# A four-layer kernel whose last layer is a recurrence: the lower layers of the first two blocks in two halves, slots by readiness, and another order of loading

## The chip, the core and the metric

The kernel runs on one core of a Trainium2 chip. The metric is the time of one launch in device microseconds; before the change the median of three runs is 1330.2 us (1329.89 to 1331.93).

## The reference

x is (8, 512, 256) in float32: 8 sequences, 512 time steps, 256 features. A condition vector of 256 features goes with each sequence. Four layers follow one another, each added to its input:

```python
x = x + moe(x, cond)         # shared silu gate unit (512 hidden) + top 2 of 8 experts (128 hidden each, gelu)
x = x + haar(x, cond)        # Haar levels, one gate per feature on all levels
x = x + adapted(x, cond)     # down, gelu, up; each with a rank-8 part that cond generates
x = x + gru(x, cond)         # h0 = cond

def gru(X, h0):              # per time step
    Z = sigmoid(x Wxz + H Whz + b);  R = sigmoid(x Wxr + H Whr + b)
    C = tanh(x Wxh + (R * H) Whh + b)
    H = Z * H + (1 - Z) * C
    Y = H Whq + bhq
```

As every level of the Haar layer has the same gate, the kernel computes that layer as one factor per sequence and feature (`lr2`). Only the recurrent layer links the time steps.

## The kernel before

**Blocks.** The 512 steps are cut into 16 windows (blocks) of 32 steps; a block of 8 sequences is 256 columns. For each block `window_jobs` adds *jobs* to lists: `hidden` (32 products of x with the first weights, two feature halves for each of 8 shared and 8 expert parts, into two PSUM banks `hp`), the sigmoid or Erf on ACT (tile `sig`, a ring of three), products on DVE (`lin`, `g`, `gl`; `gl` is a ring of three), the gate product on POOL (`g`, L594), and `into_acc` (24 products into the bank `acc`). Then come the *lower layers*: x1 on DVE (L612), x2 = x1 times `lr2` on POOL (L621), and twice `adapted`: a low-rank product into `misc` (`low_in`), the mask `u` on DVE (L649), four products with `wsq_a` and two with `low_out` into `low`; between the two an Erf on ACT (L691) and `mid` on DVE (L700). At the end x is updated on DVE (L713) and turned into `xt`, time major, by two copies on POOL (L722). Each product is a `quads` call (L453): four 32-column tiles at once, 8 matmuls.

**The order.** No scheduler on the chip chooses; the program is written out once, in order for each engine. A `Job` has an engine, the jobs that it depends on, the buffers that it uses and a planned duration (`TAKES`, `takes`, `lag` for a transfer). A `Ring` of more than one buffer gives them out only in the order in which the tiles were asked for when the jobs were made. Before the recurrence `Jobs.run` plays a clock and gives each engine the first ready job of its list `queues`. It runs until block 0's `acc`, the generated low-rank weights (`got_low_in`) and the recurrent weights (`wx`, `wh`) are there by its plan, and then until block 0's `xt` is; then `AHEAD` = 3 more PE jobs are placed.

**The prologue.** x of the first four blocks, `sw13`, `rw1`, `sw2`, `wsq_a`, `rw2`, eight pieces of `w2` (1 MB each, a ring of five buffers), `wx`, `wh` and the rest of x are loaded by the SP queue in this order. `route` computes the gates of four blocks (24 small DVE operations in a chain), which go through HBM (`comb_d`) and come back broadcast to all partitions (`bc`). A chain of small products and operations on cond makes `hid`; `generate` (L1023) multiplies it with the pieces of `w2`; a copy and a transpose on PE make `low_out` and `low_in`.

**The recurrence.** Step s writes the products of the state with `wh` (`recur`, L1115, tiles `grh` and `gz`), activations (L1281), DVE transposes (L1295), and two scans per step (L1372) that give the new state `s_h`. Between them `fill` puts jobs of the blocks to come into slots: on PE up to one job before the candidate's products (if `behind(s)` says that the plan's pace is missed, or if none are left) and one or two after them. Five steps ahead, `project` (also L1115, with `wx`) adds a group's input products; it needs `xt` of its block, and asserts that the jobs that make it have been placed. Outputs of chunks of 16 steps (`output_jobs`) are `urgent` for chunks below `HELD` = 12, and otherwise in the list `last`, which is used only when all blocks' PE jobs are placed.

```python
def behind(s, by=0):
    return (
        any(j.done is None for j in ends[1])
        or jobs.left("PE") > all_left * (LAST - s) / (LAST + LEAD) + by
    )
...
jobs.fill("PE", now + 0.5, 1 if behind(s) or late(s) else 0)
...
two = behind(s, 8) or ahead % 2 == 0 and behind(s)
jobs.fill("PE", now + 1.44, 2 if two else 1)
```

Of the kernel before, what the change touches and what calls it, by code (L numbers as in the profile page):

```python
# [50 lines left out]
LOW = (3, 2), (0, 1)  # L51
EARLY = 4
# [9 lines left out]
AHEAD = 3  # L62
# [74 lines left out]
class Jobs:  # L137


    def __init__(self):  # L140
        self.queues = {e: [] for e in TAKES}
        self.urgent = {e: [] for e in TAKES}
        self.last = {e: [] for e in TAKES}
        self.small = {e: [] for e in TAKES}
        self.clock = {e: 0.0 for e in TAKES}
        self.now = 0.0

# [9 lines left out]
    def fill(self, eng, now, most, ahead=40, then=None, of=None):  # L157

        n = 0
        while n < most:  # L160
            last = [] if self.left("PE") else self.last[eng]
# [17 lines left out]
    def run(self, until):  # L179

        while any(j.done is None for j in until):
            for eng, at in self.clock.items():
                if at <= self.now:
                    job = next((j for j in self.queues[eng] if j.ready(self.now)), None)
                    if job is not None:
                        self.queues[eng].remove(job)
# [13 lines left out]
def cond_resid_kernel(  # L200
# [69 lines left out]
    r_sig = ring("sig", [P, NT], 3)  # L270
    r_lin = ring("lin", [P, NT], 2)
    r_g = ring("g", [P, NT], 6)
    r_gl = ring("gl", [P, NT], 3)
# [36 lines left out]
    jobs = Jobs()  # L310

# [35 lines left out]
    def load_x(n, mb, some=None):  # L347
# [8 lines left out]
        a, b = (i * WS for i in some)  # L356
        for k in range(KC):
            got = load(t[:, k, :, a:b], xs[:, k, :, t0 + a : t0 + b], mb)
# [5 lines left out]
    load_x(0, 0.25, (0, 1))  # L364
    sw13_sb = const.tile([P, 2, KC, HS], F32, name="sw13_sb")
    got_sw13 = [load(sw13_sb[:, g], rows_of(sw13[g]), 0.5) for g in range(2)]
    load_x(0, 0.4, (1, EARLY))
    got_vec = load(vec, vecs, 0, eng="ACT")
    got_b2 = load(b2[: 4 * R], bias2.rearrange("q (r d) -> (q r) d", d=C), 0, eng="ACT")
    rw1_sb = const.tile([P, KC, E, P], F32, name="rw1_sb")  # L370
    got_rw1 = load(rw1_sb.rearrange("p k e h -> p k (e h)"), rows_of(rw1), 1.0)
    sw2_sb = const.tile([P, HC, C], F32, name="sw2_sb")
    got_sw2 = load(sw2_sb, rows_of(sw2), 0.5)
    wsq_a = const.tile([P, KC, 5, C], F32, name="wsq_a")
# [5 lines left out]
    r_w2 = Ring(pro.enter_context(tc.tile_pool(name="w2q", bufs=5)), "w2", [P, R * C], 5)  # L380
# [84 lines left out]
    def window_jobs(w, routed, xt, via_pool=False):  # L465
# [18 lines left out]
        def fetch(i):  # L484
# [12 lines left out]
                lag=LAG,  # L497
# [27 lines left out]
        def hidden(lazy, n, lhs, got):  # L525
            last = None
            for k in range(KC):
                last = mm(
                    lazy,
                    n,  # L530
                    lambda k=k: lhs(k),
                    lambda k=k: x[:, k],
                    k == 0,
                    [last, got, got_x[w]],
                )
            return last
# [3 lines left out]
        for m in range(HC):  # L540
            h, sig, lin, g = bank(), Lazy(r_sig), Lazy(r_lin), Lazy(r_g)
            j1 = hidden(h, 0, lambda k, m=m: sw13_sb[:, 0, k, ts(m, P)], got_sw13[0])
            j3 = hidden(h, 1, lambda k, m=m: sw13_sb[:, 1, k, ts(m, P)], got_sw13[1])
# [26 lines left out]
        for e2 in range(0, E, 2):  # L570
            h = bank()
            for n in range(2):
                e = e2 + n
                j = hidden(h, n, lambda k, e=e: rw1_sb[:, k, e, :], got_rw1)
# [15 lines left out]
                    [h, sig, gl],  # L590
                )
# [15 lines left out]
        x1, x2 = Lazy(r_x1), Lazy(r_x2)  # L607
        done = []
        for m in range(KC):
            d = add(  # L610
                "DVE",
                lambda m=m: stt(  # L612
                    bt(x1.get()[:, m]), bt(acc.get()[:, m]), THIRD, x[:, m], ALU.mult, ALU.add
                ),
                [order[0]],
                [acc, x1],
            )
# [4 lines left out]
                        x2.get()[:, m].rearrange("p (b t) -> p b t", t=WS),  # L622
                        x1.get()[:, m].rearrange("p (b t) -> p b t", t=WS),
                        lr2[:, m, :].rearrange("p (b o) -> p b o", o=1).broadcast_to([P, B, WS]),
# [3 lines left out]
                    [x1, x2],  # L628
                )
            )  # L630

        def adapted(out, n, src, base, deps, first):

            lu = Lazy(r_m)
            last = None
            for k in range(KC):
                last = mm(
                    lu,
                    0,
# [825 lines left out]
```

## Time and profile before

| what | us |
|---|---|
| median of three runs (lowest, highest) | 1330.2 (1329.89, 1331.93) |
| the profiled execution, its own time | 1334.46 |
| its span, first to last instruction | 1332.2 |
| mean granted TensorE clock | 0.984 |
| PE, DVE, ACT, POOL busy | 1183.3, 914.9, 507.3, 149.3 |
| DMA | 46.44 MB, mean 35 GB/s |

The page cuts the span into 40 equal slices and gives busy tenths of each engine and the granted clock; a timeline line gives start, duration, engine, line of the kernel, operation, tiles written and read, shape and count, and in brackets how long the engine was idle before it and what released it. A line of the windows view gives a stretch, its length, busy time with the number of instructions for PE, PE weight loads, DVE, ACT and POOL, then the granted clock, the DMA share and GB/s. Times are from the start of the span.

### The profile page before, as it was taken

What the parts mean: (1) busy time and instruction counts of PE and PEld (TensorE: products, weight loads), DVE (VectorE), ACT (ScalarE), POOL (GpSimd) and SP (SyncE); (2) the same over time, 40 slices, a digit from 0 to 9 for tenths busy, and PEclk for the clock granted to TensorE, in tenths of its full rate; (3) what the DMA queues carried; (4) which work ended last, traced back from release to release, by engine and by line L of the source; (5) the groups of instructions that cost most, each with busy time, mean ns of one, the idle gap of its engine ahead of it and who ended that gap; (6) DMA issues with size and microseconds to landing.
All of it is one profiled execution on the core that took longest, in us unless ns stands there. A gap on an engine that the chain in (4) does not pass through costs nothing.

```text
span 1332.2 us, 88576 instructions
## 1 busy us (share of the span) xinstructions
PE 1183.3 (89%) x39016; PEld 704.9 (53%) x39016; DVE 914.9 (69%) x6255; ACT 507.3 (38%) x3403; POOL 149.3 (11%) x228
## 2 busy tenths in 40 slices
PE   8999989999898998989898988888888888988885
PEld 4565555555555555555454554545454554555554
DVE  5267777777776767666676767667676766767665
ACT  2143433343343434334343434434343443433332
POOL 3310111101010110101011010101101010110000
PEclk8999999999999999999999999999999999989997
DMA  9910001101010000201000010100001000000111
GB/s 338 330 51 13 4 6 44 44 5 36 5 41 15 20 20 4 52 4 28 12 21 20 4 36 4 28 12 20 20 4 36 4 4 4 5 4 4 36 36 19
DMA packets 41586, 46.44 MB, mean 35 GB/s; under 512 B 27472, under 2 KB 31088, under 8 KB 40048
## 3 DMA queue, kind: packets, MB, share of 16 engines
q1 hardware_dynamic: 38304, 38.31, 9.6%
q8 instruction: 304, 4.98, 1.5%
q0 software_dynamic: 1184, 2.31, 0.6%
q14 instruction: 82, 0.67, 0.2%
q10 hardware_dynamic: 1712, 0.16, 0.1%
HBM read 36.45 MB, written 4.33 MB: 31 GB/s over the span
## 4 chain that ended last, share of the span: by engine, by line
PE 68%; DVE 17%; ACT 8%; issue 5%; DMA 1%; POOL 0%; DVEq 0%; ACTq 0%; POOLq 0%
PE grh L1115 34%; PE hp L453 13%; PE acc L453 8%; DVE rT L1295 6%; DVE d L1295 5%; PE gz L1115 5%; ACT r L1281 5%; PE low L453 4%; ACT c L1281 3%; PE misc L453 3%; DVE s_h L1372 2%; DVE s_rh L1312 2%; DMA brow<-in_bias_rows_dram 0%; DMA bc<-comb_d 0%; PE misc L1023 0%
## 5 line engine op out<-in xcount | busy, mean ns | idle before, releaser
L1281 ACT ACTIVATE r<-grh 128x32 f32<-128x32 f32 x1024 | 146.3, 195 | 439.8 <-PE grh L1115 439.8
L1295 DVE STREAM_TRANSPOSE rT<-r 128x32 f32<-128x32 f32 x1024 | 156.0, 190 | 225.6 <-ACT r L1281 221.6
L1115 PE MATMUL grh<-wh,s_h 128*32 128x64 f32 x8192 | 223.8, 226 | 75.4 <-DVE s_h L1372 74.2
L1115 PEld LDWEIGHTS grh<-wh,s_h 128*32 128x32 f32 x8192 | 145.0, 110 | 274.4 <-DVE s_h L1372 271.2
L1115 PE MATMUL grh<-wh,s_rh 128*32 128x64 f32 x8192 | 223.1, 227 | 52.0 <-DVE s_rh L1312 29.8
L1281 ACT ACTIVATE c<-grh 128x32 f32<-128x32 f32 x1024 | 146.3, 195 | 310.0 <-PE grh L1115 307.6
L1115 PEld LDWEIGHTS grh<-wh,s_rh 128*32 128x32 f32 x8192 | 141.6, 109 | 201.5 <-DVE s_rh L1312 198.9
L1295 DVE STREAM_TRANSPOSE d<-c 128x32 f32<-128x32 f32 x1024 | 156.5, 192 | 119.3 <-ACT c L1281 113.5
L1115 PE MATMUL gz<-wh,s_h 128*32 128x64 f32 x8192 | 212.1, 221 | 1.2 <-issue 1.2
L1115 PEld LDWEIGHTS gz<-wh,s_h 128*32 128x32 f32 x8192 | 155.3, 111 | 1.7 <-issue 1.6
L453 PE MATMUL hp<-x,sw_sb 128*32 128x256 f32 x2016 | 151.8, 389 | 1.7 <-ACT sig L546 1.1
L594 POOL TENSOR_TENSOR g<-gl,bc 128x256 f32<-128x256 f32 x128 | 93.6, 733 | 518.1 <-DVE s_h L1372 355.6
L453 PE MATMUL hp<-x,rw_sb 128*32 128x256 f32 x2016 | 149.6, 380 | 2.3 <-ACT sig L578 1.1
L453 PE MATMUL acc<-g,rw_sb 128*32 128x256 f32 x2048 | 150.2, 379 | 1.6 <-POOL g L594 1.1
L1372 DVE TENSOR_TENSOR_SCAN s_h<-d,d 128x16 f32<-128x16 f32 x1024 | 145.3, 183 | 0.0
L1312 DVE TENSOR_TENSOR s_rh<-rT,s_h 128x8 f32<-128x8 f32 x1024 | 133.1, 167 | 0.0
L1295 DVE STREAM_TRANSPOSE zT<-z 128x64 f32<-128x64 f32 x512 | 121.6, 238 | 1.1 <-ACT z L1281 1.1
L1281 ACT ACTIVATE z<-gz 128x64 f32<-128x64 f32 x512 | 121.0, 236 | 1.9 <-PE gz L1115 1.4
L1115 PE MATMUL grh<-wx,xt 128*32 128x128 f32 x2048 | 106.8, 276 | 3.3 <-ACT r L1281 3.3
L1386 ACT COPY hist<-s_h 128x16 f32<-128x16 f32 x512 | 105.9, 207 | 0.5 <-DVE s_h L1372 0.5
L1324 DVE TENSOR_TENSOR d<-zT,s_h 128x16 f32<-128x16 f32 x512 | 90.8, 177 | 17.6
L1325 DVE TENSOR_SCALAR d<-zT 128x16 f32<-128x16 f32 x512 | 86.8, 170 | 0.0
(151 smaller groups left out, 1193.4 us busy)
## 6 DMA issues: line engine op xcount, KB each, us to landing
bc<-comb_d SPq DMA_DIRECT2D x56, 256.0 KB, 3.2
w<-in_w_dram SPq DMA_DIRECT2D x8, 1024.0 KB, 12.6
out_dram<-x SPq DMA_DIRECT2D x14, 256.0 KB, 3.2
x<-in_xT_dram SPq DMA_DIRECT2D x2, 1536.0 KB
rw_sb<-in_rw_dram SPq DMA_DIRECT2D x2, 1024.0 KB
bc<-comb_d POOLq DMA_DIRECT2D x8, 256.0 KB, 8.4
sw_sb<-in_sw_dram SPq DMA_DIRECT2D x3, 512.0 KB, 6.3
wsq_a<-in_sq_a_dram SPq DMA_DIRECT2D x1, 1280.0 KB
```

Of the source, the lines that this page charges most:

```text
L453: nc.tensor.matmul(out[ts(j, 32)], lhs[:, ts(j, 32)], rhs, start=start, stop=False, skip_group_check=True,)
L594: lambda gl=gl, g=g, e=e: nc.gpsimd.tensor_tensor(g.get(), gl.get(), bcs[e // 2].get()[:, e % 2], ALU.mult),
L1115: nc.tensor.matmul(out[ts(j, 32)], lhs, rhs[:, ..., ts(j, FQ)], start=start, stop=False, skip_group_check=True,)
L1281: nc.scalar.activation(x, y, func)
L1295: ins = nc.vector.transpose(dst.rearrange("p i u b -> p i (u b)"), src.rearrange("p (i r) -> p i r", r=32),)
L1312: prod = tt(s_rh[u][:, k, u, :], rT[:, k, u, :], h[:, k], ALU.mult)
L1324: tt(d1[:, :, u, :, 1], zT[:, :, u, :], h, ALU.mult)
L1325: nc.vector.tensor_scalar(d0[:, :, :, 1], zT[:, :, u, :], -1.0, 1.0, ALU.mult, ALU.add)
L1372: new = nc.vector.tensor_tensor_scan(s_h[v][:, k, v].rearrange("p b w -> p (b w)"), d0[:, k].rearrange("p b w -> p (b w)"), d1[:, k, u].re ...
L1386: nc.scalar.copy(hist[:, :, t, :], s_h[v][:, :, v, :, 1])
```

## The change

The lower layers move to a function `lower`, called once for each part of a block: two parts of 16 steps for blocks 0 and 1 (`HALVED`), one for the others. In a half, two half-width products make one job. `window_jobs` now returns a list of ends for each part, and the recurrence starts when the first half of block 0 is planned. The Erf of the lower layers gets a ring of its own (`mid_sig`); `gl` has eight buffers instead of three; `w2` four instead of five. x of block 0 and `sw13` are loaded in turn by halves of the 256 features, `sw2` goes before `rw1`, and `rw1` comes in two loads of four experts. `hidden` waits for each half of the features by itself and starts the second bank half only after the first's k=0 product. The mean, variance and square root on cond are placed ahead of the routing. The small list, in which the routing and block 0's `gl` operations now are, is served by `run` after the main one. The planned landing times of `comb_d` and `bc` are longer. In the recurrence the two PE slots ask how many jobs are ready, and the held outputs are open once the last block's `acc` is placed.

```diff
-AHEAD = 3
+AHEAD = 1
+HALVED = 2
...
+        self.ending = lambda: not self.left("PE")
...
-            last = [] if self.left("PE") else self.last[eng]
+            last = self.last[eng] if self.ending() else []
...
-                    job = next((j for j in self.queues[eng] if j.ready(self.now)), None)
+                    qs = (self.queues[eng], self.small[eng])
+                    ready = ((j, q) for q in qs for j in q if j.ready(self.now))
+                    job, q = next(ready, (None, None))
...
+    r_mid_sig = ring("mid_sig", [P, NT], 2)
...
-    r_gl = ring("gl", [P, NT], 3)
+    r_gl = ring("gl", [P, NT], 8)
...
+    jobs.clock["PE"] = 3.5
...
-    load_x(0, 0.25, (0, 1))
-    sw13_sb = const.tile([P, 2, KC, HS], F32, name="sw13_sb")
-    got_sw13 = [load(sw13_sb[:, g], rows_of(sw13[g]), 0.5) for g in range(2)]
-    load_x(0, 0.4, (1, EARLY))
+    sw13_sb = const.tile([P, KC, 2, HS], F32, name="sw13_sb")
+    got_sw13 = []
+
+    def load_sw13(k):
+        rows = sw13[:, ts(k, P), :].rearrange("g p h -> p g h")
+        got_sw13.append(load(sw13_sb[:, k], rows, 0.5))
+
+
+    load_x(0, 0.6, (0, 1), load_sw13)
+    load_x(0, 0.5, (1, EARLY))
...
-    r_w2 = Ring(pro.enter_context(tc.tile_pool(name="w2q", bufs=5)), "w2", [P, R * C], 5)
+    r_w2 = Ring(pro.enter_context(tc.tile_pool(name="w2q", bufs=4)), "w2", [P, R * C], 4)
...
-                lag=LAG,
+                lag=2 * LAG if via_pool else LAG,
...
+            j0, j1 = hidden(h, 0, lambda k, m=m: sw13_sb[:, k, 0, ts(m, P)], got_sw13)
+            *_, j3 = hidden(
+                h, 1, lambda k, m=m: sw13_sb[:, k, 1, ts(m, P)], got_sw13, j0
+            )
...
+                    queue=None if w else jobs.small,
...
+        halves = 2 if w < HALVED else 1
+        for half in range(halves):
+            at = slice(half * WS // halves, (half + 1) * WS // halves)
+            turned.append(lower(w, at, acc, x1, x2, mid, xt, order[0]))
+        return turned
...
+        def units(products, deps, lazies):
+
+            last, made = None, []
+            step = 1 if whole else 2
+            for a in range(0, len(products), step):
+                group = products[a : a + step]
+                last = add(
+                    "PE",
+                    lambda group=group: [f() for f in group],
+                    [*deps, last],
+                    lazies,
+                )
+                made.extend([last] * len(group))
+            return made
...
-            sig = Lazy(r_sig)
+            sig = Lazy(r_mid_sig)
...
+            if w == 0 and not whole and at.start == 0 and m:
+                turned.append(
+                    add("ACT", lambda turn=turn: turn(copy=nc.scalar.copy), [d], [xt], 0.3)
+                )
+            else:
+                turned.append(
+                    add("POOL", turn, [d], [xt], TAKES["POOL"] * (0.2 + 0.8 * scale))
+                )
...
-            queue = jobs.queues if via_pool else jobs.small
-            d = jobs.add("DVE", fn, [d, got_rbias], (), takes, queue)
+            d = jobs.add("DVE", fn, [d, got_rbias], (), takes, jobs.small)
...
-        made = []
+        made, lag = [], 1.8 * LAG if via_pool else LAG
...
-            assert all(j.done is not None for j in ends[w]), g
+            of = ends[w][g * GS % WS * len(ends[w]) // WS]
+            assert all(j.done is not None for j in of), g
...
-        jobs.run(ends[0])
+        jobs.run(ends[0][0])
...
-                any(j.done is None for j in ends[1])
+                any(j.done is None for j in ends[1][0])
...
-        def late(s):
-
-            return not jobs.left("PE")
-
+        def first_slot(s, at):
+
+            if any(j.done is None for j in ends[1][0]) or jobs.ending() and jobs.left("PE"):
+                return 1
+            if jobs.left("PE"):
+                return 1 if behind(s) and jobs.ready("PE", at + 1.0) > 1 else 0
+            return 1 if len(jobs.last["PE"]) > T - s else 0
+
+        def second_slot(s, at):
+
+            if not jobs.left("PE"):
+                return 1
+            two = behind(s, 8) or (s + 5) % 2 == 0 and behind(s)
+            if two and (any(j.done is None for j in ends[1][0]) or jobs.ending()):
+                return 2
+            return 2 if two and jobs.ready("PE", at + 1.0) > 2 else 1
+
+
+        jobs.ending = lambda: l0_ends[-1].done is not None
...
-                jobs.fill("PE", now + 0.5, 1 if behind(s) or late(s) else 0)
+                jobs.fill("PE", now + 0.5, first_slot(s, now + 0.5))
...
-                two = behind(s, 8) or ahead % 2 == 0 and behind(s)
-                jobs.fill("PE", now + 1.44, 2 if two else 1)
+                jobs.fill("PE", now + 1.44, second_slot(s, now + 1.44))
```

## The prediction

> **What bounds the kernel now.** I read the page first: the span, the busy shares, the granted clock and the chain.
>
> ```profile
> span 1332.2 us, 88576 instructions
> PE 1183.3 (89%) x39016; PEld 704.9 (53%) x39016; DVE 914.9 (69%) x6255; ACT 507.3 (38%) x3403; POOL 149.3 (11%) x228
> PEclk8999999999999999999999999999999999989997
> PE 68%; DVE 17%; ACT 8%; issue 5%; DMA 1%; POOL 0%; DVEq 0%; ACTq 0%; POOLq 0%
> ```
>
> PE carries 68% of the chain, but most of its length is one thing: the serial recurrence of 512 steps. The group view of the scan (L1372, two scans a step) shows where it begins and ends.
>
> ```profile
> L1372 DVE TENSOR_TENSOR_SCAN s_h<-d,d x1024: 172/185/194, 71.1 to 1326.5; 128x16 f32<-128x16 f32 x171
> ```
>
> So there are three parts: 71.4 us to the end of the first step, 1255.3 us for the other 511, and 5.6 us of tail. In the timeline an undisturbed step takes 2.417 us (steps 223 to 455 exceed it by 0.3 us in all), and 511 x 2.417 = 1235.1, so 20.2 us are lost in steps: 11.3 in the first 128, 4.6 in the next 96, 3.9 after step 455. The floor itself is not touched by the change. What can move is the time before the recurrence and the 20.2 us.
>
> For the first I read the timeline backwards from the first recurrent product. The last two of the eight routed products g of block 0 run late on POOL:
>
> ```profile
> 30.63 2.21 POOL L485 DMA_DIRECT2D bc<-comb_d  x4 [4.78 <-DMA comb_d<-cT]
> 36.88 2.79 POOL L594 TENSOR_TENSOR g<-gl,bc 128x256 f32<-128x256 f32 x4 [4.04 <-DMA bc<-comb_d]
> 40.24 1.42 POOL L594 TENSOR_TENSOR g<-gl,bc 128x256 f32<-128x256 f32 x2 [0.56 <-DMA bc<-comb_d]
> 46.77 0.73 POOL L594 TENSOR_TENSOR g<-gl,bc 128x256 f32<-128x256 f32 x1 [2.98 <-DVE gl L586]
> 48.87 0.73 POOL L594 TENSOR_TENSOR g<-gl,bc 128x256 f32<-128x256 f32 x1 [1.37 <-DVE gl L586]
> ```
>
> The gates land at 36.9; the last g starts 12 us later, because with three gl buffers the hidden units cannot run ahead of POOL. Then come the lower layers of the whole block (acc ends at 53.5):
>
> ```profile
> 53.57 0.76 DVE L612 SCALAR_TENSOR_TENSOR x<-acc,x 128x256 f32<-128x256 f32 x2 [0.62 <-PE acc L453]
> 54.07 1.19 POOL L621 TENSOR_TENSOR x<-x,lr 128x256 f32<-128x256 f32 x2 [4.47 <-DVE x L612]
> 55.91 0.82 PE L453 MATMUL misc<-x,low_in 128*32 128x256 f32 x6
> ...
> 65.07 1.17 POOL L722 COPY xt<-x 128x256 f32<-128x256 f32 x2 [9.80 <-DVE x L713]
> ...
> 66.74 1.05 PE L453 MATMUL acc<-g,sw_sb 128*32 128x256 f32 x16
> ...
> 67.61 0.40 PE L1115 MATMUL grh<-wx,xt 128*32 128x128 f32 x8
> ...
> 68.92 0.29 PE L1115 MATMUL grh<-wh,s_h 128*32 128x64 f32 x7
> ```
>
> xt is ready at 66.2, PE is still on block 1's products until 67.6, and the first recurrent product starts at 68.92: 15.4 us after acc. A third limit lies close behind, in the DMA queue's timeline:
>
> ```profile
> 40.43 1.61 SPq L317 DMA_DIRECT2D wx<-in_sq_b_dram  x3
> 42.09 4.25 SPq L317 DMA_DIRECT2D wh<-in_sq_b_dram  x4
> ```
>
> wh takes a median 13.7 us to land, so the last of the four, issued at 45.8, is there near 59. Nothing recurrent can start before it.
>
> For the 20.2 us I cut windows at steps 141 to 143:
>
> ```profile
> 421.70:424.10 2.40, 1.29 (x59) 0.86 (x60) 1.75 (x14) 1.34 (x8) 0.00 (x0) 1.00 0.04 7
> 424.10:426.70 2.60, 2.06 (x60) 1.44 (x62) 2.12 (x15) 0.79 (x6) 0.00 (x0) 0.74 0.00 0
> 426.70:430.50 3.80, 3.80 (x90) 2.81 (x90) 2.15 (x15) 0.89 (x6) 0.00 (x0) 0.73 0.03 6
> ```
>
> One step has no filler on PE (1.29 busy of 2.40), the clock then falls to a mean of 0.74, and the next two steps take 1.5 us too long together.
>
> **The change, term by term**, against the profiled execution (1334.5 us, of which 2.3 lie around the span; it is 4.3 above the median of the runs, 1330.2).
>
> *acc of block 0 ends earlier.* With eight gl buffers all hidden units can be done before the gates land. POOL then needs 8 x 0.73 = 5.8 us from 36.9, so acc cannot end before 42.7 + 2 products x 0.43 = 43.6. PE needs, from 37.6, 16 acc products x 0.43 = 6.9, one generate of 1.73 and small ones of about 0.9: 47.1. If PE must take a second generate first and the routing slips by the eight lin/g operations now ahead of it on DVE (8 x 0.42 = 3.4; its own 24 small operations go to the list served last), it is 52. The block-1 gate fetches (4 x 0.55 on POOL) now have time before 36.9. The lower layers' split does nothing here. I take 47.1: -6.4 (-1.5 to -9.9).
>
> *acc to the first recurrent product.* Row by row, halved: the two x1 and x2 1.76 -> 1.2 (no row at 128x128; 0.42 on 128x256 and 0.19 on 128x32 put DVE at about 0.28; POOL's 0.61 lies between 0.3 and 0.61, taken 0.45); PE's queue 0.65 -> 0.4; each of two sets of eight products 3.5 -> 1.8 (the row of wx at 128 columns: 0.21 a product); Erf and mid 1.3 -> 1.1; x and xt 1.8 -> 1.2 (two engines for xt); the products ahead of the projections 1.4 -> 0.4 (one instead of three); projections 1.3. Sum 9.2 against 15.4 with its gaps. The block of memsets and the bias sum, 51.3 to 52.9 on DVE, now lies under DVE's idle time before acc ends; earlier acc puts it in the middle: +1.5 at most, I take 1. So -5.2 (-3 to -6.2).
>
> *The weights.* Both together would start the recurrence at 68.9 - 11.6 = 57.3. wh lands near 59 now. The transfers before it are the same bytes; with the generates run as soon as pieces land, the gap in which the SP queue waits for PE (two waits, 12.9 us in all, most of it hidden by transfers under way) may give up to 3. The ring of four pieces instead of five takes some of that back: nothing if the first generate follows the landing, 2.4 us (1 MB at the 421 GB/s that the windows show from 20 to 40 us) if not. I set 59 for the first product: the front term is then **-10** (-4 to -13), and wh or wx is what is late next.
>
> *Loads by chunk, conditioning ahead of routing.* They let PE begin its k=0 products with x and half of sw13. Now 48 products take 9.7 to 15.6 because the granted clock is down (0.71 over 10 to 20 us). PE does not end the front after this change, so I cost it at zero; if PE is the limit it gives up to 3, and if ACT or DVE wait in order behind it, it costs 1.
>
> *The second half of block 0, and block 1.* 14 products of block 1 are done between 53.5 and 68.9 now; fewer will be (3 to 10), and 8 half-products units are added behind the start. Steps 1 to 27 hold 3 fillers each, 81 slots, less 4 for outputs; 8 + 56 + 8 are due by step 27, where block 1 is first projected, and its lower chain leaves about 8 slots unused. That is full. Steps with three fillers show 0.06 us too much on average (1.6 us over steps 1 to 27), and a late xt stops PE, with all recurrent products behind it in its queue, for about one POOL copy and one DVE operation, 1.0 us, at steps 11, 27, 43 and 59. Bounds: 0 if everything is on time, 2.4 (one step) at each of the four. I take +2 (0 to +9).
>
> *Own Erf buffers and slots by readiness.* Sigmoids of the next block had to wait in the ring's order for the Erf of the present one, which empties PE's slots. Cures of the dips at steps 80/81, 142/143 and 206/207: 0.9 + 1.5 + 1.5 = 3.9; I take **-3** (0 to -4). The Trainium skill, "TensorE: Matmul & The Clock Gate", section Part 1, speaks against this term: it lets the clock drop only after a whole idle window of about 3.4 us. In the row above PE is 54% busy and the clock drops all the same. By the page the term would be zero.
>
> *The end.* Output products may now start before the last lower layers are done and are spread to the end: steps 457 to 459 and 508 to 511 lose 1.4 and 1.6 us at half clock. I take **-1** (+1 to -3).
>
> Sum: -10 + 2 - 3 - 1 = -12: 1322.5 for a profiled execution like this one, 1318 against the median. The 2.15 us issue stall at 203.5 and its after-effect (3.8 in all) I count neither way; it may be what puts this execution above the median.
>
> **The rivals.** (a) The front gains little: wh and wx land when they do now, the routing slips, and the first product starts at 64 to 66. For it: the DMA share is 1.0 from 10 to 68 us. Against: SP's waits on PE show slack. The front gains 3 to 5 and the rest 0 to 2: 1323 to 1327. Chance 0.18. (b) Slower: blocks 0 to 2 come late. An earlier start does not make work disappear: each of the first four half-block deadlines (steps 11, 27, 43, 59) is missed. With -14 from front, dips and end, it decides from 14 / (4 x 2.417) = 1.5 steps at each; at 2.5 steps the time is 1330 - 14 + 24 = 1340. For it: 72 due in 77 slots. Against: block 1 finishes now with about two steps to spare, and the halves' chains are shorter. Chance 0.10. (c) No change, 1328 to 1332: front 4, given back by steps 1 to 59. Chance 0.05. The forecast itself, 1309 to 1323: 0.67.
>
> **How the numbers follow.** About 0.2% (2.7 us) is what a measurement can tell from no change. Faster: 0.67 + 0.18 = 0.85; the same 0.05; slower 0.10. The range takes in the front's far bound with all of the dips and the end (1330 - 13 - 4 - 3 = 1310, and 2 more if readiness also thins the overfull steps: 1308) and reaches over rival (a) to 1328; what is left out above it is rival (b) and part of (c).
>
> **What would show it.** Right: the first scan ends at 60 to 62 instead of 71.4; POOL's eight g's follow one another from about 37; acc ends before 49; the lower layers of block 0 appear as 128x128 shapes; no step without filler in 1 to 450. Wrong: PE's first recurrent product waits for a wh or wx transfer beyond 62; PE waits for POOL's xt at steps 11, 27, 43 or 59 for over 2 us; more than 16 us lost over 2.417 per step.

## The result, and the profile after

The median falls from 1331.74 us (8 runs, 1329.89 to 1334.27) to 1325.62 us (8 runs, 1323.31 to 1327.64); the ratio is 0.995, with a 95% interval of 0.9939 to 0.9962. That is 6.1 us, half of the 12 that were forecast. The profiled execution takes 1327.38 us, with this head of the page (span, busy time, granted clock, chain by engine):

```profile
span 1325.6 us, 89001 instructions
...
PE 1183.5 (89%) x39240; PEld 690.9 (52%) x39240; DVE 915.6 (69%) x6271; ACT 505.8 (38%) x3407; POOL 150.5 (11%) x235
...
PEclk9999999999999999999999999999999999999998
...
PE 66%; DVE 19%; ACT 9%; issue 4%; DMA 1%; SPq 0%; ACTq 0%; DVEq 0%
```

PE is as busy as before; the clock's dips in the steps have gone, and the mean granted clock is 0.995 instead of 0.984. The group view of the scan marks where the recurrence begins and ends:

```profile
L1460 DVE TENSOR_TENSOR_SCAN s_h<-d,d x1024: 171/186/194, 77.6 to 1319.5; 128x16 f32<-128x16 f32 x171
```

The first step now ends at 77.9 instead of 71.4: the front, which was to give 10 us, costs 6.5. The other 511 steps lose 6.8 us over 511 x 2.417 instead of 20.2: they give 13.4 where 2 were forecast. The tail grows by 0.3. The sum, +6.5 - 13.4 + 0.3 = -6.6, is the span's difference. Two large errors of opposite sign hide in one total, so the two had to be taken apart.

**The front.** POOL's timeline (start, duration, instruction, and in brackets its idle time and releaser):

```profile
30.43 0.53 POOL L981 DMA_DIRECT2D comb_d<-cT  x1 [15.80 <-DVE cT L930]
35.24 3.83 POOL L508 DMA_DIRECT2D bc<-comb_d  x7 [4.28 <-DMA comb_d<-cT]
42.36 1.42 POOL L625 TENSOR_TENSOR g<-gl,bc 128x256 f32<-128x256 f32 x2 [3.30 <-DMA bc<-comb_d]
45.72 2.80 POOL L625 TENSOR_TENSOR g<-gl,bc 128x256 f32<-128x256 f32 x4 [1.93 <-DMA bc<-comb_d]
49.29 1.59 POOL L625 TENSOR_TENSOR g<-gl,bc 128x256 f32<-128x256 f32 x2 [0.77 <-PE acc L476]
```

All eight gl are done by 40.7, as the prediction wanted. But the gates leave DVE 5 us later (cT ends at 30.1 instead of 25.0), the broadcasts, seven in a row now, land in two groups, and the last g starts at 50.2 against 48.9. PE's timeline shows what comes after that:

```profile
50.51 0.39 PE L1095 MATMUL misc<-w,hid 128*32 128x256 f32 x2
54.02 3.20 PE L1095 MATMUL misc<-w,hid 128*32 128x256 f32 x26 [3.13 <-DMA w<-in_w_dram]
56.59 0.64 PE L476 MATMUL acc<-g,rw_sb 128*32 128x256 f32 x2
57.01 0.55 PE L1095 MATMUL misc<-w,hid 128*32 128x256 f32 x2
57.02 1.40 PE L476 MATMUL acc<-g,rw_sb 128*32 128x256 f32 x14
58.35 0.44 PE L1120 MATMUL grh<-ident,low_out 128*128 128x128 f32 x2
58.72 3.66 PE L476 MATMUL acc<-g,rw_sb 128*32 128x256 f32 x64
62.20 1.48 PE L476 MATMUL hp<-x,sw_sb 128*32 128x256 f32 x24
```

The fourth generate has begun and stands for a piece of w2 whose last part lands just before 54.0. Ten acc products (80 matmuls, of five g's that are all there by 50.9) stand behind it in PE's order, and acc ends at 62.4. The stop costs more than its 3.13 us. The windows view of the stop and of what follows it:

```profile
50.90:54.00 3.10, 0.00 (x0) 0.00 (x0) 0.00 (x0) 0.00 (x0) 0.51 (x1) 0.99 1.01 376
54.00:57.40 3.40, 3.38 (x35) 1.59 (x38) 0.00 (x0) 0.00 (x0) 0.00 (x0) 0.51 1.10 202
```

The granted clock is halved for 3.4 us behind the stop, and the 26 matmuls of the row at 54.02 take 3.20 us; in e2 below, at a clock of 1.00, the same 26 take 1.70. From there to the recurrence (rows of DVE, POOL and PE together, in order of time):

```profile
62.45 0.88 DVE L681 SCALAR_TENSOR_TENSOR x<-acc,x 128x128 f32<-128x128 f32 x4 [1.91 <-PE acc L476]
...
70.97 0.41 POOL L791 COPY xt<-x 128x128 f32<-128x128 f32 x1 [6.67 <-DVE x L784]
...
71.84 0.28 PE L1188 MATMUL grh<-wx,xt 128*32 128x128 f32 x2
...
74.30 0.43 PE L1188 MATMUL grh<-wx,xt 128*32 128x128 f32 x8 [1.78 <-issue]
...
75.29 0.43 PE L1188 MATMUL grh<-wh,s_h 128*32 128x64 f32 x16
```

The halves do shorten this chain: xt is there 9.1 us after x1 begins, against 12.7 before. Then 1.78 us pass in which PE waits for nothing that the profile shows.

**The steps.** The windows view, at steps 141 to 143 of the kernel after:

```profile
420.70:423.10 2.40, 2.40 (x76) 1.45 (x80) 1.48 (x12) 0.91 (x7) 0.62 (x1) 1.00 0.00 0
423.10:425.50 2.40, 2.04 (x76) 1.08 (x80) 1.76 (x13) 0.79 (x6) 0.00 (x0) 1.00 0.03 7
425.50:427.90 2.40, 2.40 (x84) 1.49 (x85) 2.08 (x13) 0.79 (x6) 0.00 (x0) 1.00 0.00 0
```

Each of the three has its filler products and the clock stays at 1.00, where before had 1.29 busy of 2.40 in step 141 and a clock of 0.74 behind it. The same view of the last six steps, before and then after:

```profile
1310.60:1318.10 7.50, 3.84 (x172) 2.90 (x176) 4.72 (x35) 2.37 (x18) 0.00 (x0) 0.88 0.03 5
1318.10:1326.70 8.60, 5.35 (x160) 4.12 (x160) 4.76 (x35) 2.67 (x19) 0.00 (x0) 0.50 0.01 2
```

```profile
1304.80:1312.00 7.20, 5.63 (x204) 3.02 (x204) 5.05 (x37) 2.36 (x18) 0.00 (x0) 1.00 0.34 44
1312.00:1319.70 7.70, 4.79 (x192) 3.63 (x192) 4.91 (x38) 2.46 (x18) 0.00 (x0) 0.82 0.02 4
```

Before, PE was 51% busy in the first three of them (3.84 of 7.50), the clock then fell to 0.50, and the last three took 8.6 us. After, output products held for these steps keep it up nearly to the end.

### The profile page after: what moved, and what is told of

It is laid out like the page before. It is cut to its first block, busy times and chain, and to the rows that moved or that the text cites. A ratio compares the mean times of both kernels' runs of the same rounds, so it can differ in the third digit from the quotient of the medians.

```text
span 1325.6 us, 89001 instructions
## 1 busy us (share of the span) xinstructions
PE 1183.5 (89%) x39240; PEld 690.9 (52%) x39240; DVE 915.6 (69%) x6271; ACT 505.8 (38%) x3407; POOL 150.5 (11%) x235
## 4 chain that ended last, share of the span: by engine, by line
PE 66%; DVE 19%; ACT 9%; issue 4%; DMA 1%; SPq 0%; ACTq 0%; DVEq 0%
PE grh L1188 35%; PE hp L476 11%; DVE d L1384 7%; PE acc L476 6%; DVE rT L1384 6%; PE gz L1188 5%; ACT c L1370 5%; PE low L476 5%; ACT r L1370 4%; PE misc L476 3%; DVE s_h L1460 3%; DVE s_rh L1401 2%; DMA w<-in_w_dram 1%; PE misc L1095 1%; DMA sw_sb<-in_sw_dram 0%
## 5 line engine op out<-in xcount | busy, mean ns | idle before, releaser
L1188 PEld LDWEIGHTS grh<-wh,s_h 128*32 128x32 f32 x8192 | 141.0, 109 | 309.4 <-DVE s_h L1460 308.2
L476 PE MATMUL acc<-g,rw_sb 128*32 128x256 f32 x2048 | 155.1, 380 | 0.2 <-issue 0.2
## 6 DMA issues: line engine op xcount, KB each, us to landing
w<-in_w_dram SPq DMA_DIRECT2D x8, 1024.0 KB, 12.7
```

The costliest lines, as they stand in the source:

```text
L476: nc.tensor.matmul(out[ts(j, 32)], lhs[:, ts(j, 32)], rhs, start=start, stop=False, skip_group_check=True,)
L1188: nc.tensor.matmul(out[ts(j, 32)], lhs, rhs[:, ..., ts(j, FQ)], start=start, stop=False, skip_group_check=True,)
```

## The experiments

All numbers at once. "x1" is the start of the first operation on acc's sum, "first" the first recurrent product, "lost" what 511 steps take over 2.417 us each; these and the span are from one profiled execution. The ratio is that of the timed runs to the runs of before on the same chip.

| kernel | x1 | first | lost | tail | span | median | ratio [95%] |
|---|---|---|---|---|---|---|---|
| before | 53.6 | 68.9 | 20.2 | 5.6 | 1332.2 | 1331.74 | |
| after | 62.4 | 75.3 | 6.8 | 5.9 | 1325.6 | 1325.62 | 0.9950 [0.9939, 0.9962] |
| e1_whole | 61.5 | 77.0 | 7.0 | 5.9 | 1327.6 | 1329.88 | 0.9972 [0.9961, 0.9983] |
| e2_ring5 | 54.9 | 70.8 | 6.3 | 5.9 | 1321.6 | 1323.52 | 0.9928 [0.9910, 0.9945] |
| e3_route | 58.2 | 74.1 | 6.5 | 5.9 | 1324.2 | 1325.70 | 0.9946 [0.9925, 0.9966] |
| e4_ring_route | 57.0 | 72.3 | 9.7 | 5.9 | 1326.1 | 1325.71 | 0.9945 [0.9925, 0.9965] |
| e5_sig_slots | 53.9 | 69.5 | 5.6 | 5.5 | 1318.4 | 1321.28 | 0.9921 [0.9907, 0.9936] |
| e6_half_old_front | 55.7 | 73.4 | 7.9 | 5.5 | 1325.2 | 1324.80 | 0.9947 [0.9927, 0.9966] |
| e7_sig_only | 53.6 | 69.1 | 12.3 | 5.6 | 1324.7 | 1325.31 | 0.9948 [0.9932, 0.9965] |
| e8_old_slots | 61.5 | 72.6 | 8.4 | 5.9 | 1324.6 | 1328.03 | 0.9969 [0.9956, 0.9982] |
| e9_ring4 | 54.8 | 70.4 | 7.2 | 6.4 | 1321.7 | 1325.47 | 0.9943 [0.9925, 0.9960] |
| e10_small_list | 59.0 | 74.3 | 7.4 | 5.5 | 1325.0 | 1325.49 | 0.9953 [0.9938, 0.9968] |
| e11_chunks | 55.9 | 70.9 | 5.7 | 7.5 | 1321.9 | 1323.24 | 0.9929 [0.9902, 0.9956] |
| e12_cond_first | 56.6 | 72.2 | 6.8 | 6.3 | 1323.0 | 1324.76 | 0.9937 [0.9914, 0.9960] |
| e13_gl5 | 56.1 | 72.2 | 7.2 | 5.6 | 1322.8 | 1323.45 | 0.9918 [0.9895, 0.9940] |
| e14_gl8_ring4 | 56.6 | 72.1 | 7.8 | 5.9 | 1323.6 | 1325.59 | 0.9939 [0.9917, 0.9961] |
| e15_ahead0 | 54.3 | 69.1 | 8.1 | 5.6 | 1320.4 | 1323.30 | 0.9923 [0.9898, 0.9947] |
| e16_ahead6 | 53.8 | 71.4 | 7.6 | 6.0 | 1322.6 | 1323.95 | 0.9922 [0.9900, 0.9943] |
| e17_hidden_first | 51.2 | 70.0 | 6.8 | 5.6 | 1320.0 | 1323.06 | 0.9923 [0.9907, 0.9940] |
| e18_hidden_first_gl3 | 51.1 | 69.9 | 7.2 | 6.1 | 1320.8 | 1322.03 | 0.9910 [0.9895, 0.9925] |

### One part of the change undone

**e1_whole**: the halves off, everything else as after.

```diff
-HALVED = 2
+HALVED = 0
```

> The changed kernel with the lower layers of blocks 0 and 1 in one part again (all else as changed). In the changed kernel's profile the first step ends at 77.9 us instead of 71.4, and 6.8 us are lost in the steps instead of 20.2. Theory A (the split itself shortens the front; what made the front late lies before acc): from acc to the first projection 9.5 us become about 14, the first step ends at 81 to 83, and the time is 3 to 5 us longer than the changed kernel's, about 1330; the loss in steps stays at 5 to 9. Rival B (the split brings nothing or costs, as the half units and the second half stand in PE's queue): the first step ends at 78 or before, and the time is 1326 or less.

From x1 to the first product it takes 15.5 us, against 12.8 in the kernel after and 15.4 before. The halves are worth 2.6 us here, or 4.4 without the issue stall of 1.78. acc is as late as after, so the loss in the front isn't theirs.

**e2_ring5**: five w2 buffers. They fit with five gl buffers, not with eight, and more PE jobs have to be placed ahead, since an earlier start leaves block 1 too late in the plan. **e3_route**: the routing back on the main list. **e4_ring_route**: both.

```diff
-AHEAD = 1
+AHEAD = 4
-    r_gl = ring("gl", [P, NT], 8)             # e2, e4
+    r_gl = ring("gl", [P, NT], 5)
-    r_w2 = Ring(... bufs=4)), "w2", [P, R * C], 4)   # e2, e4
+    r_w2 = Ring(... bufs=5)), "w2", [P, R * C], 5)
-            d = jobs.add("DVE", fn, [d, got_rbias], (), takes, jobs.small)   # e3, e4
+            queue = jobs.queues if via_pool else jobs.small
+            d = jobs.add("DVE", fn, [d, got_rbias], (), takes, queue)
```

> The changed kernel with five w2 buffers again, gl with five buffers to make room, and four PE jobs placed ahead instead of one (1.3 us of PE before the start at most). Theory A (the ring of four made the front late: the generates wait for w2 inside PE's queue until 56.6, and block 0's last acc products stand behind them): the last generate ends by 51, acc ends at 55 to 57 instead of 62.3, the first step ends at 71 to 73, the time is 4 to 7 us below the changed kernel's, 1319 to 1322. Rival B (the late routing is the limit, gates at 42.4 instead of 36.9): acc still ends at 59 or later, time within 2 us of the changed kernel's.

> The changed kernel with block 0's routing operations in the main list of DVE again, and four PE jobs placed ahead instead of one. Theory A (the ring of w2 is the limit): the gates land 4 to 5 us earlier, at 37 to 39, but the last generate still waits for w2 to about 56 and acc ends at 60 or later: time within 2 us of the changed kernel's. Rival B (the routing is the limit): acc ends at 57 to 58, the first step at 73, the time is 4 to 5 us below, 1321.

> Both of the two: five w2 buffers (gl five), routing in DVE's main list, four PE jobs placed ahead. If the two are separate limits one behind the other, both together bring the front below that of the kernel before: acc ends at 50 to 52, wh lands at 57 to 59, the first step ends at 64 to 67, and with 7 to 9 us lost in the steps the time is 1312 to 1316. If the front is limited by something else (loads by chunk, wh), the first step ends at 71 or later and the time is 1319 or more.

x1 comes 7.5 us earlier with the fifth w2 buffer (and five gl buffers), 4.2 with the routing on the main list, 5.4 with both: each is a cause, and they don't add. In e2 the fourth generate starts at 45.5 instead of 50.3, which is 4.8 of the 7.5. It still stops for its piece, but 1.1 us less, and the clock stays at 1.00, which is nearly all of the rest. In e3 and e4 the granted clock is 0.50 for 6.8 us from about 24, which it isn't in e2 or in the kernel after; what that cost them was not measured. The last generate ends at 50.0, 53.7 and 52.1 instead of 57.6. With the routing on the main list the first g starts at 36.1 instead of 42.4, but the last one at 55.2, as its hidden unit is late again. In e2 a second thing is seen in PE's timeline, below the row of the fourth generate; xt is there at 65.0:

```profile
48.13 1.70 PE L1095 MATMUL misc<-w,hid 128*32 128x256 f32 x26 [2.02 <-DMA w<-in_w_dram]
...
65.02 1.06 PE L476 MATMUL low<-x,wsq_a 128*32 128x128 f32 x32
...
66.76 1.05 PE L476 MATMUL acc<-g,sw_sb 128*32 128x256 f32 x16
67.62 1.05 PE L476 MATMUL hp<-x,sw_sb 128*32 128x256 f32 x16
68.49 0.61 PE L476 MATMUL misc<-mid,low_in 128*32 128x128 f32 x8
68.93 0.27 PE L1188 MATMUL grh<-wx,xt 128*32 128x128 f32 x1
```

3.9 us pass between xt and the first projection, filled with the second half's products and block 1's, which are ahead of it in PE's order. xt comes 6.6 us earlier than in the kernel after, the first recurrent product 4.5.

**e8_old_slots**: the old rule for the slots and the held outputs, the rest as after.

```diff
-        jobs.ending = lambda: l0_ends[-1].done is not None
...
-                jobs.fill("PE", now + 0.5, first_slot(s, now + 0.5))
+                jobs.fill("PE", now + 0.5, 1 if behind(s) or not jobs.left("PE") else 0)
...
-                jobs.fill("PE", now + 1.44, second_slot(s, now + 1.44))
+                two = behind(s, 8) or ahead % 2 == 0 and behind(s)
+                jobs.fill("PE", now + 1.44, 2 if two else 1)
```

> The changed kernel with the old slot rule (first slot by pace alone, held outputs only when nothing else is left) and its own Erf ring kept. Theory A (slots by readiness give 5 us or more of the steps' gain): 11 to 15 us lost in steps, the time is 4 to 8 us above the changed kernel's. Rival B (the Erf ring is the main cause): 9 us or less lost, within 2 us of the changed kernel's.

The steps from 455 to the end lose 4.0 us again (after 0.6, before 3.9); those from 0 to 455 lose 4.3 (after 6.1). The slot rule is worth the end, and little before it. By the timed runs alone e8 and the kernel after can't be told apart: their intervals overlap.

### Parts of the change alone, on the kernel before

**e7_sig_only**: only the Erf's own ring. **e5_sig_slots**: that, `first_slot`, `second_slot` and the early end, with no halves and the front of before.

```diff
+    r_mid_sig = ring("mid_sig", [P, NT], 2)
...
-            sig = Lazy(r_sig)
+            sig = Lazy(r_mid_sig)
```

> The kernel before with the Erf ring of its own and nothing else. Theory A (the emptied slots and the clock dips after them come from the shared ring, and are 4 to 5 us of the 13): dips at steps 80/81, 143 and 207 are gone, 14 to 17 us lost in steps, the time is 3 to 6 us below the kernel before. Rival B (the ring is the main cause): 9 us or less lost, time 10 us or more below. Rival C (clock dips move elsewhere): 19 us or more lost, no change.

> The kernel before with only two parts of the change: the Erf ring of its own and the slots by readiness (with the held outputs opened after the last acc); front, loads, rings and undivided lower layers as before. Theory A (the loss in steps falls from 20.2 to 6.8 us by these two alone, whatever the front does): the first step ends at 71 to 72 as before, 6 to 9 us are lost in the steps, and the time is 10 to 13 us below the kernel before. Rival B (the steps gain because of the new front, eight gl buffers or the halves): 13 us or more are lost, the time is 3 to 7 us below.

Steps 43 to 223 lose 13.7 us before, 4.6 in e7 and 2.7 in e5; steps 455 to 511 lose 3.9, 4.4 and 0.1. The ring alone takes 7.9 of 20.2 away, the slot rule another 6.7, of which 4.2 at the end. The last six steps in e7 and then in e5, in the windows view:

```profile
1302.60:1310.50 7.90, 4.45 (x172) 3.34 (x174) 4.74 (x35) 2.46 (x18) 0.00 (x0) 0.73 0.01 3
1310.50:1319.10 8.60, 5.39 (x160) 4.16 (x160) 4.76 (x36) 2.65 (x18) 0.00 (x0) 0.50 0.01 2
```

```profile
1298.30:1305.60 7.30, 5.74 (x204) 3.12 (x208) 5.15 (x38) 2.36 (x18) 0.00 (x0) 1.00 0.35 45
1305.60:1312.80 7.20, 4.16 (x192) 2.90 (x192) 4.81 (x37) 2.36 (x18) 0.00 (x0) 1.00 0.01 3
```

e5 beats both kernels: its interval lies below that of the kernel after. What the change gains over before is in these two parts.

**e6_half_old_front**: e5 with the halves, and five PE jobs placed ahead.

```diff
-AHEAD = 3
+AHEAD = 5
-HALVED = 0
+HALVED = 2
```

> As the one before, with the halves of blocks 0 and 1 as well and five PE jobs placed ahead instead of three; loads, routing, w2 and gl rings still as before. Theory A (the split shortens acc to xt by 3 to 4 us, and only the new loading and routing made the front late): acc ends at 53 to 54, xt of the first half is there at 62 to 63, the first step ends at 67 to 70, 6 to 10 us are lost in steps, the time is 1316 to 1319. Rival B (the earlier start is given back at the deadlines of blocks 0 and 1): 12 us or more lost in steps, mostly before step 59, time 1321 or more.

xt is there at 66.0 in place of 67.6, but the first projection starts at 72.1 instead of 67.9: 6.1 us of PE's order, 1.6 of them an issue stall, stand between. Halves on the old front, with the five jobs placed ahead that they came with, gain nothing: the ratio is higher than e5's, though the intervals just overlap.

### The pieces of the new front, one at a time on e5

**e9_ring4**: four w2 buffers. **e10_small_list**: the routing and block 0's gl on the small list, five gl buffers. **e11_chunks**: x, sw13 and rw1 by chunk. **e12_cond_first**: e11, with the conditioning ahead of the routing and the longer landings.

```diff
-    r_w2 = Ring(... bufs=5)), "w2", [P, R * C], 5)        # e9
+    r_w2 = Ring(... bufs=4)), "w2", [P, R * C], 4)
...
+                    queue=None if w else jobs.small,      # e10, gl
-            queue = jobs.queues if via_pool else jobs.small
-            d = jobs.add("DVE", fn, [d, got_rbias], (), takes, queue)
+            d = jobs.add("DVE", fn, [d, got_rbias], (), takes, jobs.small)
...
+    load_x(0, 0.6, (0, 1), load_sw13)                     # e11, e12
+    load_x(0, 0.5, (1, EARLY))
```

> The kernel of the own Erf ring and the slots by readiness, with the front of before (first recurrent product at 69.5, span 1318.4, x1 starts at 53.9), and as its only edit four w2 buffers instead of five. Theory (the ring of four makes the last generates wait in PE's queue): the last generate ends at 54 to 58 instead of 50.0, x1 starts at 58 to 62, the first product at 73 to 77, span 1322 to 1326. Rival (the transfers are the same bytes and the ring only shifts issues): last generate within 1 us of 50.0, first product 69 to 70.5, span 1318 to 1320.

> The same base, with the routing and block 0's gl operations on the small list, served after the main one, and five gl buffers instead of three; five w2 buffers as before. Theory (the list served last delays the gates, and the larger ring gives back only a part): the last routing operation ends at 27 to 30 instead of 25, the first g starts at 39 to 42.5 instead of 36.9, x1 starts at 55 to 58, first product 71 to 73, span 1320 to 1322. Rival (the gates are not what acc waits for once gl has five buffers): x1 at 50 to 54, first product 66 to 69.5, span 1315 to 1318.5.

> The same base, with x of block 0 and sw13 loaded in turn by feature halves, sw2 ahead of rw1 in two loads, and the hidden products waiting for each half by itself; five w2 buffers as before, routing and conditioning where they were. Theory (PE does not end the front, as the prediction had it): first product 68.5 to 70.5, span 1317.5 to 1319.5. Rival (PE is late from its first products on and everything follows): first product 66.5 to 68.5, span 1315.5 to 1317.5. Other rival (x of blocks 1 to 3, which the routing needs, lands after sw13 and the routing slips): first product 71 to 73, span 1320 to 1322.

> The kernel with loads by chunk, and besides it the mean, variance and square root on cond ahead of the routing, and the planned landing of comb_d and bc later; routing on the main list, three gl and five w2 buffers. Theory (the conditioning ahead of the routing delays the gates by its own DVE time, under 2 us, and lets the generates start no earlier, since they wait for w2): first product 69.5 to 72, span 1318.5 to 1321. Rival (the generates start earlier by what the conditioning gains and acc with them): first product 66 to 68.5, span 1315 to 1317.5.

None of them gains. x1 is 0.9, 5.1, 2.0 and (with e11's) 2.7 us later than in e5. Not all of that need be the piece's own: the granted clock is at 0.50 for 3.4 us in e10 (from 46.2) and e11 (from 29.9) and for 6.8 us in e12 (from 23.5), and in e9 and e5 in none of the front after 16.3. My theory of the ring fell: alone it costs 0.9, not 4 to 8, as here the last piece lands at 49.7 and not at 54.0, and the clock stays at 1.00 behind PE's stop of 1.84 us. Only where the pieces are asked for later (in the kernel after the first three generates start 2.1 to 3.4 us later than in e9) does the ring's last landing come behind everything else. The small list is the dearest piece; POOL's timeline of e10:

```profile
32.92 0.53 POOL L924 DMA_DIRECT2D comb_d<-cT  x1 [19.85 <-DVE cT L873]
36.92 2.22 POOL L490 DMA_DIRECT2D bc<-comb_d  x4 [3.47 <-DMA comb_d<-cT]
45.20 4.91 POOL L600 TENSOR_TENSOR g<-gl,bc 128x256 f32<-128x256 f32 x7 [6.06 <-DMA bc<-comb_d]
```

The routing ends 6.7 us later than in e5 (32.6, not 25.9), more than the theory had, and the seven g's do then follow one another: it is the gates that acc now waits for.

### What the forecast rested on

**e13_gl5** and **e14_gl8_ring4**: on e5, a larger gl ring.

```diff
-    r_gl = ring("gl", [P, NT], 3)
+    r_gl = ring("gl", [P, NT], 5)       # e13; 8 in e14, which has four w2 buffers
```

> The kernel of the own Erf ring and the slots by readiness with the front of before (acc's end seen by x1 at 53.9, last g at 49.0, first product 69.5), and as its only edit five gl buffers instead of three. Theory of the prediction (three gl buffers hold the hidden units back, so the last g's are late): last g at 43 to 46, x1 at 48 to 51, first product 64 to 67, span 1313 to 1316. Rival (PE, with the generates and hidden products in its order, is what the last g waits for): last g at 47.5 to 49.5, x1 at 53 to 54.5, first product 68.5 to 70, span 1317.5 to 1319.

> The same base with eight gl and four w2 buffers, routing and gl operations on the main list. The ring of four alone gave x1 at 54.8 and the first product at 70.35. Theory of the prediction: x1 at 47 to 51, first product 62.5 to 67, span 1312 to 1316. Rival: x1 at 53 to 56, first product 69 to 71.5, span 1318 to 1321.

The prediction's theory of the gl ring falls. In e14, POOL's and then PE's timeline:

```profile
35.45 4.18 POOL L597 TENSOR_TENSOR g<-gl,bc 128x256 f32<-128x256 f32 x6 [1.96 <-DMA bc<-comb_d]
47.95 0.73 POOL L597 TENSOR_TENSOR g<-gl,bc 128x256 f32<-128x256 f32 x1 [6.16 <-issue]
49.99 0.72 POOL L597 TENSOR_TENSOR g<-gl,bc 128x256 f32<-128x256 f32 x1 [1.31 <-DVE gl L589]
```

```profile
44.52 1.70 PE L1068 MATMUL misc<-w,hid 128*32 128x256 f32 x26 [1.17 <-DMA w<-in_w_dram]
45.85 0.39 PE L456 MATMUL hp<-x,rw_sb 128*32 128x256 f32 x2
46.05 0.39 PE L1068 MATMUL misc<-w,hid 128*32 128x256 f32 x2
46.06 0.59 PE L456 MATMUL hp<-x,rw_sb 128*32 128x256 f32 x4
...
47.87 1.07 PE L456 MATMUL hp<-x,rw_sb 128*32 128x256 f32 x16
```

With eight buffers six g's follow one another once the gates land, and the last two still start at 48.0 and 50.0: their hidden products stand behind the third generate in PE's order. e13's x1 is later than in e5, too, and there the clock has a part. The second generate in e13 and then in e5:

```profile
38.63 3.38 PE L1068 MATMUL misc<-w,hid 128*32 128x256 f32 x32
```

```profile
38.24 1.91 PE L1068 MATMUL misc<-w,hid 128*32 128x256 f32 x32
```

The granted clock is 0.50 from 38.2 to 41.6 in e13 and 1.00 in e5. A fall to 0.50 near 38 is there in e6, e17 and e18, too, and not in before, e7, e15 and e16, with the same loads: differences of less than 2 us in the front of single profiles carry no weight.

**e15_ahead0** and **e16_ahead6**: on e5, another number of PE jobs placed ahead.

```diff
-AHEAD = 3
+AHEAD = 0       # e15; 6 in e16
```

> The same base with no PE job placed ahead between the planned end of xt and the first projections, instead of three. Theory (the three run under the wait for xt, which ends 0.3 us before the first projection, and cost nothing): first product 69 to 70, span 1318 to 1319.5, losses in steps 0 to 59 within 1 us of 2.6. Rival (they hold the first projection up): first product 67.5 to 68.8, span 1316.5 to 1318.

> The same base with six PE jobs placed ahead instead of three. Theory (what is placed behind the three stands after xt and each costs its own time of 0.43 us, in PE's order): first product 70.5 to 71.5, span 1319 to 1321, and nothing comes back in the steps, which have slots enough. Rival (they fit under the wait for xt too): first product 69 to 70, span 1317.5 to 1319. Far rival (a placed job waits for another engine and holds PE longer than it takes): first product 72 to 74, span 1321 to 1324.

None ahead: the first product comes 0.4 earlier, and steps 0 to 59 lose 4.1 instead of 2.6; by these two profiles the three are better done ahead. Six: 2.0 later, or 0.65 for each added job, and nothing comes back. By the ratios the three kernels can't be told apart.

**e17_hidden_first** and **e18_hidden_first_gl3**: block 0's last hidden and all its acc products ahead of the third and fourth generate, with five and with three gl buffers.

```diff
+        to_here = len(jobs.queues["PE"])      # ahead of the second pair's generates
...
-    ends = [window_jobs(w, routed, xts[w], True) for w in range(2)]
+    to_there = len(jobs.queues["PE"])
+    ends = [window_jobs(0, routed, xts[0], True)]
+    q = jobs.queues["PE"]
+    q[:] = q[:to_here] + q[to_there:] + q[to_here:to_there]
+    ends.append(window_jobs(1, routed, xts[1], True))
...
-AHEAD = 3
+AHEAD = 5
```

> The kernel of the own Erf ring and the slots by readiness with the front of before, and in PE's order the last hidden products and all acc products of block 0 ahead of the third and fourth generate; five gl buffers, five PE jobs placed ahead of the first projection (three leave block 1 late in the plan). Theory (the place behind the third generate is what the last two g's wait for): last g at 41 to 45 instead of 49.0, x1 at 46 to 50 instead of 53.9, third and fourth generate at 44 to 51, xt at 60 to 64.5, and since the jobs placed ahead then stand behind xt, first product 65 to 68.5, span 1314 to 1318. Rival (the second low_in, or w2's landing near 48 to 50, is what comes next): x1 as above, xt 65 to 67.5, first product 68.5 to 71, span 1318 to 1321.

> The same with three gl buffers. Theory (the gl ring was never the limit, the place in PE's order was): x1, xt and first product within 1 us of the kernel with five buffers. Rival (with the products moved up, three gl buffers do hold the last two back, since POOL must read two gl first): x1 later by 1.5 to 4 us, first product by as much.

The size of the gl ring makes no difference (x1 51.2 and 51.1, first product 70.0 and 69.9). x1 is 2.7 us earlier, less than expected, since the last g still starts at 48.7 (in both the clock was at 0.50 for 3.4 us from about 38). And the gain is gone by the first product: both generates now stand between x1 and the lower layers' products (51.4 to 55.0), xt is there at 66.5, and the placed jobs follow. e18 has the lowest ratio of all, but its interval covers e5's ratio.

## Why the prediction was wrong about the front, and too small about the steps

**acc of block 0: -6.4 forecast, +8.9 measured.** This step failed, in three ways, and with it the front term: -10 forecast, +6.5 measured. First, its reading of the trace: the last two g's were put down to the three gl buffers. POOL did wait for gl, and DVE's gl for POOL's g, but behind that lay PE's order (e13, e14, e17, e18: no gain by any gl ring). Secondly, a second generate ahead of the products and a late routing (acc at 52) were taken for the far end, and both slipped further. The slip of 3.4 was worked out for eight lin and g operations; it was 5.1 in the kernel after and 6.7 in e10, as idle waits in DVE's order (1.03 and 0.82 us for PE's products) come on top of the operations. Thirdly, the ring of four, priced at 0 or 2.4, was priced as a delay of transfers. In the kernel after it was a stop of PE, with the ten acc products behind the stopped generate and half the clock after it (e2: 7.5 us). By itself, with the pieces asked for in time, it costs 0.9 (e9).

**acc to the first product: -5.2 forecast, -2.5 measured**; 1.8 of what is missing is the issue stall. The chain itself was right: xt comes 3.5 us sooner after x1, and e1 confirms that the halves do it. The step left out what stands in PE's order between xt and the projection.

**The weights** landed at 64.0 (the last part of wh; 59.7 before), and weren't the limit. The bound of 59 was never reached by the rest.

**The loads by chunk at zero**: +1.5 us of first product in e11, just beyond the cost of 1 that was allowed. With the clock at 0.50 for 3.4 us of that front it is no more than one profile can be off by.

**Blocks 0 to 2 in time: +2 forecast.** In the steps it didn't come: steps 0 to 59 lose 2.7 us instead of 6.4, and as 3.8 of the 6.4 are the stall at 203.5 and its after-effect, without it they lose about the same (2.6). A price was paid elsewhere. Where xt came earlier (e2, e6, e17), four or five jobs were placed ahead to have block 1 in time by the plan, and in e2 and e6 3.9 and 6.1 us of PE's order stand between xt and the first projection. So a part of an earlier xt is lost again, which is near to rival (b)'s mechanism, at another place. How much of it must be lost stays open: in no run did the first product come earlier than before's 68.9.

**Erf's own ring and the slots: -3 forecast; the end: -1.** The mechanism was right and the size wrong. I counted three dips (3.9 us) that I had cut windows for, and not the whole stretch that one cause could reach: of the 13.7 us lost in steps 43 to 223 the ring took 9.1 away (e7). That includes the stretch of the stall at 203.5 us, which I had left out; whether the stall would have come anyway can't be told, but e7's timed ratio (6.9 us of 1331.5) fits its trace (7.5 us of span). The end gives 3.2 after and 3.8 in e5, where I had taken 1 of 3.

**The page on the clock.** The Trainium skill, "TensorE: Matmul & The Clock Gate", Part 1, would have made the dips and the end worth nothing without an idle window of about 3.4 us. The windows above disagree: PE is 51% busy over 7.5 us, its longest wait for another engine in that stretch is 0.79 us, and the clock halves. A long stop and a fall do go together in the front (3.13 us in the kernel after), but after 1.62 us in e13 the clock fell as well, and after 2.02 in e2 it didn't. The same page's section "A second HAM failure mode: psum-queue depth-cycling" tells of short idle times that make the clock swing, which is nearer to these rows.

Of the rivals, (a) came nearest to the time (1323 to 1327) and was wrong in its reason: it had the front gain 3 to 5 and the rest 0 to 2. That the total came out at half of the forecast is no merit of the sum: an error of 16.5 us in the front met one of 11.4 the other way in the steps. Open is what the issue stalls are (1.78 us in the kernel after, 1.63 in e6, 0.4 at most in e2); no run was aimed at them.

## What to carry to other kernels

A releaser in the trace is the last wait, not the cause: before pricing a larger ring, follow the late tile back to its products and look at what stands ahead of them in their engine's order, since an engine that stops for one transfer also holds the work behind it (here a stop of 3.13 us held ten acc products). Where the front runs into a loop that is already full, work placed ahead can eat a part of an earlier start, so price the two together. Before a difference between two fronts is put down to an edit, compare their granted clock. And where one cause empties slots, price it by all that is lost in the stretch that it can reach, not by the dips that were looked at.

## What the runs showed of the hardware

The TensorE clock fell to 0.50 with PE 51% busy and no wait for another engine over 0.79 us (3.84 of 7.50, before), and stayed at 1.00 through steps with PE 58% busy (4.16 of 7.20, the last steps of e5; it fell 0.6 us after them). The length of one wait did not decide it: the clock fell behind a wait of 1.62 us (e13) and stayed behind one of 2.02 (e2). One fall of 3.4 us made a generate of 32 matmuls take 3.38 us instead of 1.91. With the same loads in the same order it came in some profiled executions and not in others.
